# A graph layer on one core: the order of fills, stores, loads and tests in the head of the kernel

## The chip, the core and the metric

The kernel runs on one core of one Trainium2 chip. A core has five engines that each work through their own list of instructions in order: TensorE (PE in the profile), VectorE (DVE), ScalarE (ACT), GpSimd (POOL) and SyncE (SP). SP, ACT and POOL also issue DMA transfers; an issue that has to wait holds up everything behind it in its engine's list. The metric is the device time of one execution in microseconds (us). Three runs of the kernel before gave 2591.33, 2595.76 and 2597.96 us: median 2595.76.

## The reference

There are 12500 nodes with 64 features and 212500 edges, sorted by their node dst (E = 212500, N = 12500). Cut to what matters:

```
h = max(layernorm(x), 0)
e = silu(concat(h[src], h[dst], w) @ eW1 + eb1)     # an edge: 129 inputs, 128 outputs
e = silu(e @ eW2 + eb2)
agg = segment_sum(e, src, 12500)
out = x + silu(concat(h, agg) @ nW1 + nb1) @ nW2 + nb2
```

The first product is split: h @ eW1[:64] and h @ eW1[64:128] are formed once per node. The kernel calls the first table A (`ta`, by the node src, in three bf16 parts) and the second B (`tb`, by the node dst, in f32).

## The kernel before, in words

**Two halves that run beside each other.** The edges are dealt to 100 buckets by src (`NB`; bucket = src mod 100, 125 nodes each). The *sending* half takes the edges in their own order, in blocks of 1024 (208 blocks), forms for each the B row plus weight and bias (a product of a one-hot matrix `pick` with a window `win` of B's rows, lines 341 to 356), and scatters the rows to DRAM tensors `q` by bucket: eight indirect DMAs a block, issued by POOL (line 370), 1661 in all. The *step* half reads `q` bucket by bucket (line 415), adds the rows of A (line 420), does both layers and the sums per node (lines 438 to 516). The blocks are grouped in eleven chunks (`CHUNKS`); chunk 0 has eight blocks, each other chunk twenty. A chunk has its own tensor `q`, and the steps of a chunk start when all its blocks are sent. Unused places of `q` must read zero; `fill` (line 91) writes them from the tile `zeros` (line 88), in four transfers a chunk, issued by ACT at line 100.

**Order.** The order of PE, DVE, ACT and SP is the order of the code (`manual_schedule`); only POOL's is not. Work that shall run side by side is written as generators that give way after each piece. `turns(todo, 3)` runs up to three of them in turn. `send_all(c)` (line 381) sends a chunk: for each block s it loads for s + 2, issues a fill of the next chunk while there are any, and then takes three pieces of `count(s + 1)` and `send(s)` together. After each piece of chunk 0 the loop around it takes four steps of `feed`: twelve a block.

**Loads of a block (SP).** `load_rows(s)` loads `bc` (line 265; the dst row of each edge, one row broadcast to 64 partitions) and `bb` (line 267; the bucket of each edge) from the tensor `rows`. `load(s)` first calls `load_rows(s + 1)` and then loads the two halves of the window `win` (line 281), at rows that SP reads from `base_i`. `weights(s)` loads the edge weights into a row of `pick` (line 292), after DVE has written the rest of `pick`. `count(s)` (DVE) makes `pick` and the one-hot `oh` (lines 306, 307) and the running counts (lines 317, 322); `send(s)` has PE's products, two copies to `qs` by ACT (line 356), the targets `to` by DVE (line 361), and the scatters.

**The head**, before the first block is sent (lines 711 to 745):
- SP loads `x0` (the first 2048 rows of x) and `srcR`; ACT loads `dstR`.
- ACT issues the first of four fills of chunk 0; the other three are issued one after each of the next pieces of `norm(x0)` (lines 532 to 544: mean, `cen`, Square on ACT, var, Sqrt on ACT, then max and scale), `destinations()` (`f` from `dstR` by ACT, line 619; `lo`; `rowsS`; a store to `rows`, line 632) and `sources()` (`sf` from `srcR` by ACT, line 642; the bucket by DVE, lines 644 to 647; a second store to `rows`, line 650).
- `load_rows(0)`; then the transposes of the buckets to `bkE` and `first_rows(g)` four times: the rows of B of the first 2048 nodes, copied to `got` (line 183, three buffers) and stored to `tb0` by SP (line 565). Block windows below 30 read `tb0`.
- `scale(0)` (lines 670 to 673) turns buckets into target rows for chunk 0.
- `load(0)`, `load(1)`, the transposes of `locE`, and then all of `count(0)` with `weights(0)`.
- `feed` is `checks()` and after it `turns(groups(), 3)`. `checks()` tests that each window holds all rows that its block needs (lines 679 to 683, two reduces over `f`) and then scales the buckets of chunks 1 to 10, one `scale(c)` each: twelve steps in all. `groups()` makes A and B for all nodes, twelve buckets at a time: `loaded` (line 570, x into `xs`), `normed` (the norm above), and `products` of four buckets each.

Of the kernel before, what the change touches and what calls it, by code (L numbers as in the profile page):

```python
# [46 lines left out]
G = 4  # L47
# [12 lines left out]
def tile_gnn(ctx: ExitStack, tc: tile.TileContext, x, src, dst, ew, eW1, eb1, eW2, eb2, nW1, nb1, nW2, nb2, out):  # L60
# [25 lines left out]

    most_zeros = max((cap * P - zero) * G * W // 64 for _, cap, zero in CHUNKS)
    zeros = const.tile([P, most_zeros], F32, name="zeros")
    nc.gpsimd.memset(zeros, 0.0)

    def fill(c, engine, each):

# [71 lines left out]

    ta = dram.tile([P * NB, 3 * H], BF16, name="ta")
    tb = dram.tile([P * NB, H], F32, name="tb")
    rows = dram.tile([NP, 2, 2, BLK], BF16, name="rows")

    tb0 = dram.tile([P * NE, H], F32, name="tb0")
    ta_buckets, tb_buckets = (t.rearrange("(l b) f -> l b f", b=NB) for t in (ta, tb))  # L170
# [68 lines left out]
    with ExitStack() as work:  # L239
# [18 lines left out]
        def load_rows(s):  # L258

            if s < nblocks:  # L260
                p, g = s // 2, s % 2
                r = rows[p, g]
                bc = ld.tile([P, HALF], BF16, name="bc")
                of = bass.AP(tensor=r.tensor, offset=r.offset, ap=[[HALF, 2], [0, HB], [1, HALF]])
                nc.sync.dma_start(bc, of)
                bb = ld.tile([P, BLK], BF16, name="bb")
                nc.sync.dma_start(bb[:112], bass.AP(tensor=r.tensor, offset=r.offset + BLK, ap=[[0, 112], [1, BLK]]))
                blk[s] = [bc, bb]

        def load(s):  # L270

            load_rows(s + 1)
            if s < nblocks:
                p, g = s // 2, s % 2
                win = wins[s % NW]
                table, end = (tb0, NE * P) if s < EARLY else (tb, N)
                assert s < EARLY or len(done_b) == NB // G
                for a in range(2):
                    h = 2 * g + a
                    at = nc.sync.value_load(base_i[:, h, p : p + 1], min_val=0, max_val=end - WL)  # L280
                    nc.sync.dma_start(win[a * HB : a * HB + WL, :], table[bass.ds(at, WL), :])
                pick = ld.tile([P, HALF], F32, name="pick")
                blk[s] += [win, pick]

        def weights(s):

# [45 lines left out]
        def send(s):  # L332

            p, g = s // 2, s % 2
            c = chunk_of[s]
            _, _, cap, _, q = chunks[c]
            _, _, win, pick, run = blk.pop(s)
# [14 lines left out]
            halves = []  # L352
            for t0 in range(0, nt, G):
                qs = qsp.tile([P, G, W], F32, name="qs")
                m = min(G, nt - t0)
                nc.scalar.copy(qs[:, :m, :H], qps[t0 // G][:, :m, :])  # L356
                halves.append((t0, m, qs))
            for t0, m, qs in halves:
                if t0 == 0:
                    to = top.tile([P, TB], I32, name="to")  # L360
                    nc.vector.scalar_tensor_tensor(
                        to[:, :nt], rank[:, :nt], float(G * cap * P), bkE[:, g * TB : g * TB + nt, p], op0=OP.min, op1=OP.add
                    )
                at = g * TB + t0
                nc.scalar.copy(
                    qs[:, :m, H:], locE[:, at : at + m, p][:, :, None].to_broadcast([P, m, W - H])
                )
                for t in range(t0, t0 + m):
                    k = min(P, n - t * P)
                    i = nc.gpsimd.indirect_dma_start(  # L370
                        out=q[:],
                        out_offset=bass.IndirectOffsetOnAxis(ap=to[:k, t : t + 1], axis=0),
                        in_=qs[:k, t - t0, :],
                        in_offset=None,
                    )
# [182 lines left out]
        def first_rows(g):  # L558

            hr = turned(x0, g)  # L560
            yield
            got = fp.tile([P, G, H], F32, name="got")
            product(1, hr, mm, "mm", got)
            yield
            nc.sync.dma_start(tb0.rearrange("(p j) f -> p j f", j=NE)[:, g : g + G, :], got)
            yield

        def loaded(b0, n, xs):
# [48 lines left out]
        def destinations():  # L617

            nc.scalar.copy(f, dstR)
            lim = lp.tile([NP, 1], F32, name="lim")  # L620
            nc.vector.tensor_scalar(lim, part[:NP], EARLY / 2 - 0.5, float(N - NE * P), op0=OP.is_gt, op1=OP.mult)
            nc.vector.tensor_scalar(lim, lim, float(NE * P - WL), None, op0=OP.add)
            yield
            nc.vector.tensor_scalar(lo, fv[:, :, 0], lim, None, op0=OP.min)
            for g in range(2):
                nc.vector.tensor_tensor(
                    rowsS[:, g, 0, :].rearrange("p (a e) -> p a e", a=2),
                    fv[:, 2 * g : 2 * g + 2, :],
                    lo[:, 2 * g : 2 * g + 2, None].to_broadcast([NP, 2, HALF]),
                    op=OP.subtract,  # L630
                )
            nc.sync.dma_start(rows[:, :, 0, :], rowsS[:, :, 0, :])
            yield
            lot = mm.tile([1, 4, NP], F32, name="lot", tag="mm")
            for g in range(4):
                nc.tensor.transpose(lot[:, g, :], lo[:, g : g + 1], ident[:NP, :NP])
            nc.scalar.copy(base_i, lot)
            yield

        def sources():  # L640
# [6 lines left out]
            nc.vector.scalar_tensor_tensor(sf, t, -float(NB), sf, op0=OP.mult, op1=OP.add)  # L647
            yield
            nc.scalar.copy(rowsS[:, :, 1, :], sf.rearrange("p (g e) -> p g e", g=2))
            nc.sync.dma_start(rows[:, :, 1, :], rowsS[:, :, 1, :])  # L650
            yield

        def by_edges(of, to):
# [8 lines left out]
                    nc.scalar.copy(to[:, k0 : k0 + 4, :], tr)  # L662
                yield

        def scale(c):
            p0, p1, cap, _, _ = chunks[c]
            v = bkE[:, :, p0:p1]

            q4 = lp.tile([P, 2 * TB, p1 - p0], F32, name="q4", tag=f"q4{c > 0}")
            nc.vector.tensor_scalar(q4, v, 0.5 - G / 2, 1.0 / G, op0=OP.add, op1=OP.mult)  # L670
            nc.vector.tensor_scalar(q4, q4, float(3 * 2**22), None, op0=OP.add)
            nc.vector.tensor_scalar(q4, q4, -float(3 * 2**22), None, op0=OP.add)
            nc.vector.scalar_tensor_tensor(v, q4, float(cap * P * G - G), v, op0=OP.mult, op1=OP.add)

        def checks():

# [4 lines left out]
                nc.vector.tensor_scalar(ends[:, i, :], ends[:, i, :], sign, limit, op0=OP.mult, op1=OP.is_gt)  # L681
                yield
            nc.vector.tensor_reduce(bad[:NP, 0:1], ends.rearrange("p i g -> p (i g)"), AX.X, OP.max)
            for c in range(1, len(chunks)):
                scale(c)
                yield

        def groups():
# [5 lines left out]
            for i, b0 in enumerate(starts):  # L694
                if i + 2 < len(starts):
                    todo.append((b0, loaded(*of[i + 2])))
                todo += [(b0, products(b0, g, of[i][2])) for g in range(0, size(b0), G)]
                if i + 1 < len(starts):
                    todo.insert(len(todo) - size(b0) // G + 1, normed(*of[i + 1]))
            return todo  # L700

        done_a, done_b, ready = [], [], set()
# [9 lines left out]
        with tc.tile_pool(name="lists", bufs=1, side="right") as lp:  # L712
# [12 lines left out]
                    queue.dma_start(to[p0:p1, :], vec(v, p0 * PAIR, p1 - p0, PAIR))  # L725
                queue.dma_start(to[NP - 1 : NP, :LAST], vec(v, (NP - 1) * PAIR, 1, LAST))
            nc.scalar.dma_start(dstR[NP - 1 : NP, LAST:], vec(dst, E - PAD, 1, PAD))
            zero_fills = list(fill(0, nc.scalar, 7))
            zero_fills.pop(0)()
            steps_ = [norm(x0, NE), destinations(), sources()]  # L730
            for _ in turns(steps_, 3):
                if zero_fills:
                    zero_fills.pop(0)()
            load_rows(0)
            counting = count(0)
            for i, _ in enumerate(turns([by_edges(sf, bkE)] + [first_rows(g) for g in range(0, NE, G)], 3)):
                if i == 8:
                    scale(0)
            for i in range(2):
                load(i)  # L740
            for _ in by_edges(t, locE):
                pass
            for _ in counting:
                pass
            feed = itertools.chain(checks(), turns(groups(), 3))
            for _ in send_all(0):
                for _ in range(4):
                    next(feed, None)
# [203 lines left out]
```

## Time and profile before

| what | value |
|---|---|
| three runs | 2591.33, 2595.76, 2597.96 us (median 2595.76) |
| the profiled execution | 2590.2 us |
| its span | 2588.4 us, 60017 instructions |
| PE, DVE, ACT, POOL busy, share of the span | 85%, 79%, 48%, 67% |
| first scatter of block 0, 1, 2 | 63.71, 83.64, 97.01 us |
| last scatter | 2339.2 us |
| bytes moved by DMA | 577.23 MB, 223 GB/s over the span |
| POOL idle ahead of scatters, "issue" | 397.5 us in 1302 waits |
| DVE's `to` waiting for scatters | 149.3 us in 81 waits |

A line of the timeline gives start and length in us, the engine (a q behind it marks a DMA issue or the like by that engine's sequencer), the source line, the operation, the tile written and the tiles read, the shapes, a count, and in brackets the idle time of the engine just before with what ended it. A line of the waits gives who waited for what: us in total, times, and the longest. A line of busy time by stretch gives the stretch, its length, the busy us of PE, weight load, DVE, ACT and POOL with instruction counts, the clock granted to PE, the busy share of the DMA engines, and GB/s.

### The profile page before, as it was taken

Reading aid. Unit: us, or ns where it says so; the run is one execution under the profiler, and the core shown is the slowest. Engines: PE = TensorE matmul, PEld = TensorE weight load, DVE = VectorE, ACT = ScalarE, POOL = GpSimd, SP = SyncE. Lnnn points to the kernel's source line nnn. Section 1 sums busy time; section 2 is a strip of 40 time slices with the busy share of each in tenths; the row PEclk is TensorE's granted clock in tenths of the full one; section 3 lists DMA queues with packets and bytes.
Section 4 is the critical chain, followed back from the end, with each engine's and each line's share of the span. In section 5 each row is a group of like instructions: output and inputs, shape, how many; then the busy total and the mean of one; then the engine's idle time right before and its main releaser. Section 6 shows DMA issues by size and latency. Waiting matters only on the chain.

```text
span 2588.4 us, 60017 instructions
## 1 busy us (share of the span) xinstructions
PE 2205.0 (85%) x21814; PEld 2041.8 (79%) x21814; DVE 2034.8 (79%) x3464; ACT 1246.9 (48%) x2687; POOL 1736.8 (67%) x1729
## 2 busy tenths in 40 slices
PE   2456777988998998999899799889889999997997
PEld 1345667977987987888788799889879889996996
DVE  5877987987987887888788799879879889973442
ACT  2344634544554554555455455445545455553443
POOL 3675777777777777777677777777767777772000
PEclk7556888998999999999999899999989999998999
DMA  8787778669768767866966877786696667655441
GB/s 202 216 246 263 254 234 271 217 204 269 237 210 247 252 219 227 267 216 218 272 227 211 240 248 237 220 260 228 211 274 228 215 203 235 230 169 174 166 150 54
DMA packets 257977, 577.23 MB, mean 223 GB/s; under 512 B 51202, under 2 KB 110580, under 8 KB 257469
## 3 DMA queue, kind: packets, MB, share of 16 engines
q1 hardware_dynamic: 185096, 384.91, 45.7%
q0 software_dynamic: 54144, 123.04, 13.1%
q10 hardware_dynamic: 18434, 65.37, 11.4%
q8 instruction: 175, 2.87, 0.5%
q14 instruction: 128, 1.04, 0.1%
HBM read 361.44 MB, written 211.67 MB: 221 GB/s over the span
## 4 chain that ended last, share of the span: by engine, by line
PE 40%; DMA 23%; DVE 13%; POOL 7%; issue 6%; ACT 2%; SPq 1%; DVEq 0%; ACTq 0%; POOLq 0%
DMA q<-qs,to 14%; PE seg L505 10%; PE p L491 9%; POOL q L370 7%; PE pt L459 7%; PE pt L452 5%; DVE misc L317 5%; PE qp L349 4%; PE lr L438 3%; DMA bc<-rows 2%; DVE oneT L443 2%; DMA bb<-rows 2%; DVE one L472 2%; DMA pick<-in_edge_weight_dram 2%; DVE own L322 2%
## 5 line engine op out<-in xcount | busy, mean ns | idle before, releaser
L370 POOL DMA_INDIRECT q<-qs,to x1661 | 1697.4, 1022 | 602.7 <-issue 397.5
L463 ACT ACTIVATE e<-pt 128x512 f32<-128x512 f32 x525 | 313.7, 598 | 835.8 <-PE pt L459 769.6
L505 PE MATMUL seg<-one,e 128*128 128x125 f32 x4200 | 581.4, 282 | 54.7 <-DVE aggT L516 42.5
L491 PE MATMUL p<-w,e 128*128 128x128 f32 x4200 | 587.2, 284 | 5.3 <-ACT p L485 5.3
L317 DVE TENSOR_TENSOR_SCAN misc<-oh,misc 100x342 f32<-100x342 f16 (+1 forms) x623 | 579.7, 930 | 9.3 <-PE misc L341 1.2
L505 PEld LDWEIGHTS seg<-one,e 128*128 128x128 f32 x4200 | 524.4, 196 | 68.5 <-ACT p L485 27.7
L491 PEld LDWEIGHTS p<-w,e 128*128 128x128 f32 x4200 | 527.9, 197 | 31.0 <-issue 8.4
L443 DVE TENSOR_SCALAR oneT<-lr,part 125x512 bf16<-125x512 f32 x525 | 390.8, 744 | 111.1 <-PE lr L438 109.0
L459 PE MATMUL pt<-oneT,a 125*128 125x256 bf16 (+1 forms) x3300 | 443.0, 273 | 0.1
L452 PE MATMUL pt<-ident,qt 128*128 128x128 f32 x2100 | 332.0, 282 | 73.4 <-DVE oneT L443 73.4
L356 ACT COPY qs<-qp 128x512 f32<-128x512 f32 x416 | 229.2, 587 | 320.3 <-PE qp L349 225.7
L472 DVE TENSOR_TENSOR one<-nodes,qt 128x500 f32<-128x500 f32 x525 | 351.7, 670 | 0.7 <-PE seg L505 0.5
L459 PEld LDWEIGHTS <-a 125*128 125x128 bf16 x3300 | 318.7, 100 | 35.5 <-issue 1.0
L322 DVE TENSOR_TENSOR own<-misc,oh 100x342 f16<-100x342 f32 (+1 forms) x623 | 320.0, 514 | 21.6
L495 ACT ACTIVATE e<-p 128x512 f32<-128x512 f32 x525 | 314.1, 598 | 18.6 <-PE p L491 18.0
L485 ACT COPY p<-b2f 128x512 f32<-128x512 f32 x525 | 312.5, 595 | 0.1
L349 PE MATMUL qp<-win,pick 50*128 50x128 f32 x3322 | 260.7, 299 | 60.6 <-DMA pick<-in_edge_weight_dram 34.5
L349 PEld LDWEIGHTS qp<-win,pick 50*128 50x128 f32 x3322 | 220.4, 200 | 92.9 <-issue 71.5
L452 PEld LDWEIGHTS pt<-ident,qt 128*128 128x128 f32 x2100 | 228.3, 144 | 79.0 <-DVE oneT L443 76.3
L516 DVE TENSOR_TENSOR aggT<-aggT,seg 128x500 f32<-128x500 f32 x250 | 166.9, 667 | 94.2 <-PE seg L505 93.9
L438 PE MATMUL lr<-identb,qt 128*125 128x128 bf16 x2100 | 213.3, 225 | 30.6 <-DMA qt<-q 25.3
L438 PEld LDWEIGHTS <-qt 128*125 128x125 bf16 x2100 | 186.4, 139 | 42.1 <-DMA qt<-q 31.5
(121 smaller groups left out, 1086.3 us busy)
## 6 DMA issues: line engine op xcount, KB each, us to landing
qt<-q SPq DMA_DIRECT2D x250, 576.0 KB
a<-ta SPq DMA_DIRECT2D x275, 384.0 KB
q<-zeros ACTq DMA_DIRECT2D x30, 1638.0 KB
bb<-rows SPq DMA_DIRECT2D x208, 224.0 KB
bc<-rows SPq DMA_DIRECT2D x208, 128.0 KB
q<-qs,to POOLq DMA_INDIRECT x1661
win<-tb SPq DMA_DIRECT2D x416, 24.0 KB
ta<-parts SPq DMA_DIRECT2D x25, 384.0 KB
```

The lines of the kernel that those rows point to most:

```text
L317: nc.vector.tensor_tensor_scan(run[:, :m], oh[:, cols], nil.to_broadcast([NB, m]), carry.get(c, -1.0), op0=OP.add, op1=OP.add)
L322: nc.vector.tensor_tensor(own[:, cols], run[:, :m], oh[:, cols], op=OP.mult)
L349: nc.tensor.matmul(qps[a][:, t, :], pick[half, t * P : (t + 1) * P], win[half, :], start=True, stop=True)
L370: i = nc.gpsimd.indirect_dma_start(out=q[:], out_offset=bass.IndirectOffsetOnAxis(ap=to[:k, t : t + 1], axis=0), in_=qs[:k, t - t0, :], in ...
L438: nc.tensor.matmul(lr[:L, t, :], loc[:, at : at + 1].to_broadcast([P, L]), identb, start=True, stop=True)
L443: nc.vector.tensor_scalar(oneT, st[k].pop("lr")[:L], part1[:L, :], None, op0=OP.is_equal)
L452: nc.tensor.matmul(pt[:, t, :], qt[:, j, :H], ident, is_transpose=True, start=t == 0, stop=False, skip_group_check=True)
L459: nc.tensor.matmul(pt[:, cols, :], a3[:L, b, i, :], oneT[:, cols, :], start=False, stop=i == 2, skip_group_check=True)
L472: nc.vector.tensor_tensor(one.rearrange("p (b j) l -> p b j l", j=n), nodes1[:, None, None, :].to_broadcast(wide), loc[:, tiles[0][1] : ti ...
L491: nc.tensor.matmul(p2[:, t, :], e1[:, t, :], w2, start=False, stop=t == G - 1, skip_group_check=True)
L495: nc.scalar.activation(e2, p2, AF.Silu)
L505: nc.tensor.matmul(item[2][:, b, :], e2[:, t, :], one[:, t, :], start=j < G, stop=j >= G * (n - 1))
```

## The change

It has these parts:
1. `zeros` is set by VectorE instead of GpSimd.
2. The four fills of chunk 0 are all issued by ACT ahead of the norm of `x0`.
3. The rows of B of the first nodes (`tb0`) are stored by ACT instead of SP.
4. The tensor `rows` becomes two: `dests` (read as `bc`) and `bucks` (read as `bb`).
5. `load(s)` loads the window first and calls `load_rows(s + 1)` after it, in every block. In the head, all of `count(0)`, with `weights(0)`, now comes between `load(0)` and `load(1)`.
6. `checks()` is no longer ahead of the groups of nodes, but one of their generators, queued behind the products of the first twelve buckets. The ten scales of chunks 1 to 10 become one (those chunks have the same capacity), with one point at which it gives way: four steps instead of twelve. An assertion at build time makes sure that a chunk is scaled before it is sent.

```diff
-    nc.gpsimd.memset(zeros, 0.0)
+    nc.vector.memset(zeros, 0.0)
...
-    rows = dram.tile([NP, 2, 2, BLK], BF16, name="rows")
+    dests = dram.tile([NP, 2, BLK], BF16, name="dests")
+    bucks = dram.tile([NP, 2, BLK], BF16, name="bucks")
...
         def load(s):
-            load_rows(s + 1)
             if s < nblocks:
...
                     nc.sync.dma_start(win[a * HB : a * HB + WL, :], table[bass.ds(at, WL), :])
                 pick = ld.tile([P, HALF], F32, name="pick")
                 blk[s] += [win, pick]
+            load_rows(s + 1)
...
         def first_rows(g):
...
-            nc.sync.dma_start(tb0.rearrange("(p j) f -> p j f", j=NE)[:, g : g + G, :], got)
+            nc.scalar.dma_start(tb0.rearrange("(p j) f -> p j f", j=NE)[:, g : g + G, :], got)
...
-            nc.sync.dma_start(rows[:, :, 0, :], rowsS[:, :, 0, :])
+            nc.sync.dma_start(dests, rowsS[:, :, 0, :])
...
-            nc.sync.dma_start(rows[:, :, 1, :], rowsS[:, :, 1, :])
+            nc.sync.dma_start(bucks, rowsS[:, :, 1, :])
...
-        def scale(c):
-            p0, p1, cap, _, _ = chunks[c]
+        def scale(cs):
+            p0, p1, cap = chunks[cs[0]][0], chunks[cs[-1]][1], chunks[cs[0]][2]
             v = bkE[:, :, p0:p1]
-            q4 = lp.tile([P, 2 * TB, p1 - p0], F32, name="q4", tag=f"q4{c > 0}")
+            q4 = lp.tile([P, 2 * TB, p1 - p0], F32, name="q4", tag=f"q4{cs[0]}")
             nc.vector.tensor_scalar(q4, v, 0.5 - G / 2, 1.0 / G, op0=OP.add, op1=OP.mult)
             nc.vector.tensor_scalar(q4, q4, float(3 * 2**22), None, op0=OP.add)
+            yield
             nc.vector.tensor_scalar(q4, q4, -float(3 * 2**22), None, op0=OP.add)
             nc.vector.scalar_tensor_tensor(v, q4, float(cap * P * G - G), v, op0=OP.mult, op1=OP.add)
+            scaled.update(cs)
...
         def checks():
...
-            for c in range(1, len(chunks)):
-                scale(c)
+            for _, cs in itertools.groupby(range(1, len(chunks)), lambda c: chunks[c][2]):
+                yield from scale(list(cs))
                 yield
...
         def groups():
...
+                if i == 0:
+                    todo.append(checks())
...
-            zero_fills = list(fill(0, nc.scalar, 7))
-            zero_fills.pop(0)()
-            steps_ = [norm(x0, NE), destinations(), sources()]
-            for _ in turns(steps_, 3):
-                if zero_fills:
-                    zero_fills.pop(0)()
+            for f_ in fill(0, nc.scalar, 7):
+                f_()
+            for _ in turns([norm(x0, NE), destinations(), sources()], 3):
+                pass
             load_rows(0)
             counting = count(0)
...
-                    scale(0)
-            for i in range(2):
-                load(i)
+                    list(scale([0]))
+            load(0)
+            for _ in counting:
+                pass
+            load(1)
             for _ in by_edges(t, locE):
                 pass
-            for _ in counting:
-                pass
-            feed = itertools.chain(checks(), turns(groups(), 3))
+            feed = turns(groups(), 3)
             for _ in send_all(0):
                 for _ in range(4):
                     next(feed, None)
```

More of the change, by code (lines that the diff above doesn't have):

```diff
@@ L261, in load_rows @@
                 p, g = s // 2, s % 2
-                r = rows[p, g]
+                r, r2 = dests[p, g], bucks[p, g]
                 bc = ld.tile([P, HALF], BF16, name="bc")
@@ L266, in load_rows @@
                 bb = ld.tile([P, BLK], BF16, name="bb")
-                nc.sync.dma_start(bb[:112], bass.AP(tensor=r.tensor, offset=r.offset + BLK, ap=[[0, 112], [1, BLK]]))
+                nc.sync.dma_start(bb[:112], bass.AP(tensor=r2.tensor, offset=r2.offset, ap=[[0, 112], [1, BLK]]))
                 blk[s] = [bc, bb]
         def load(s):
-            load_rows(s + 1)
             if s < nblocks:
@@ L336, in send @@
             _, _, cap, _, q = chunks[c]
+            assert c in scaled
             _, _, win, pick, run = blk.pop(s)
@@ L699, in groups @@
                     todo.insert(len(todo) - size(b0) // G + 1, normed(*of[i + 1]))
+                if i == 0:
+                    todo.append(checks())
             return todo
-        done_a, done_b, ready = [], [], set()
+        done_a, done_b, ready, scaled = [], [], set(), set()
         feeding = ExitStack()
```

## The prediction

> **What bounds the kernel now.** I read the page's busy times first, then its costliest groups, then busy time by stage, then the timeline of the head.
>
> ```profile
> PE 2205.0 (85%) x21814; PEld 2041.8 (79%) x21814; DVE 2034.8 (79%) x3464; ACT 1246.9 (48%) x2687; POOL 1736.8 (67%) x1729
> ...
> L370 POOL DMA_INDIRECT q<-qs,to x1661 | 1697.4, 1022 | 602.7 <-issue 397.5
> ```
>
> POOL looks loosely used at 67%. But nearly all of it is 1661 scatters of 1.02 us, and two thirds of its idle time is "issue": about 0.30 us ahead of each scatter for which nothing in the profile is to blame. One scatter therefore holds POOL 1.32 us. The stretches (columns: length, then PE, PEld, DVE, ACT, POOL busy with counts, PE clock, DMA share, GB/s):
>
> ```profile
> 82.70:155.70 73.00, 46.93 (x347) 37.76 (x349) 64.08 (x113) 37.78 (x103) 54.04 (x51) 0.50 0.77 235
> 155.70:254.00 98.30, 50.78 (x455) 43.77 (x453) 63.70 (x108) 44.42 (x112) 60.00 (x57) 0.60 0.81 252
> 254.00:2340.00 2086.00, 1861.26 (x18943) 1739.81 (x18941) 1762.74 (x2980) 1040.78 (x2235) 1575.43 (x1545) 0.96 0.73 232
> 2340.00:2588.00 248.00, 228.09 (x1951) 205.89 (x1951) 95.34 (x157) 103.18 (x204) 19.03 (x26) 0.96 0.43 140
> ```
>
> From 254 us on, 1545 instructions x 1.32 fill 2040 of 2086 us: POOL is full, and a microsecond by which the scatters start earlier or later there stays to the end. So the change is worth what it does to the scatters of the head. Three lines of POOL's timeline (start, length, [idle before, what ended it]) are the first scatters of blocks 0, 1 and 2:
>
> ```profile
> 63.71 1.05 POOL L370 DMA_INDIRECT q<-qs,to  x1 [23.73 <-ACT qs L365]
> 83.64 1.22 POOL L370 DMA_INDIRECT q<-qs,to  x1 [9.92 <-DVE var L543]
> 97.01 0.96 POOL L370 DMA_INDIRECT q<-qs,to  x1 [3.01 <-ACT qs L365]
> ```
>
> Then blocks 3 to 8 follow at 10.6 to 11.1 us without a gap (108.10, 118.79, 129.58, 140.63, 151.73). What each part touches, from the timeline of all engines:
>
> ```profile
> 12.35 1.06 ACT L536 ACTIVATE x<-cen 128x1024 f32<-128x1024 f32 x1 [0.84 <-DVE cen L535]
> 15.66 2.32 ACTq L100 DMA_DIRECT2D q<-zeros  x1
> 18.08 1.90 ACT L642 CAST sf<-srcR 104x2048 f32<-104x2048 int32 x1 [0.54 <-issue]
> 39.41 4.77 SPq L565 DMA_DIRECT2D tb<-got  x4
> 43.17 0.65 ACT L183 COPY got<-ab 128x256 f32<-128x256 f32 x2 [7.51 <-DMA tb<-got]
> 55.86 0.60 SPq L292 DMA_DIRECT2D pick<-in_edge_weight_dram  x1
> 77.16 0.95 DVE L532 TENSOR_REDUCE mean<-xs 128x12 f32<-128x768 f32 x1 [2.82 <-DMA xs<-in_x_dram]
> 104.46 0.16 DVE L361 SCALAR_TENSOR_TENSOR to<-misc,bkE 128x8 int32<-128x8 f32 x1
> ```
>
> **Zeros on VectorE.** 936 numbers a row. The nearest DVE row, srcR's 492 in 0.47 us, gives 0.9 us; DVE then idles 7.4 us for x, which hides it (0.9 us if that cover were gone). srcR's own memset, and the two small pieces of src behind it, come 0.9 us later; the 768 KB piece does not wait for it. POOL gains 0.88 us and idles 23.7 us ahead of its first scatter. Zero.
>
> **All four fills ahead of the norm.** The first goes at 9.47, when the loads have begun to land; the others stand between ACT's steps and take 0.58, 0.61 and 2.32 us to issue. The DMA engines are full meanwhile:
>
> ```profile
> 10.00:15.00 5.00, 0.00 (x0) 0.00 (x0) 4.67 (x15) 3.72 (x4) 1.75 (x4) 1.00 1.02 257
> 25.00:30.00 5.00, 3.51 (x20) 3.20 (x22) 1.18 (x1) 3.39 (x5) 2.64 (x6) 1.00 1.00 208
> ```
>
> With a share of 1.0 from 5 to 35 us, the bytes cannot land sooner for being asked for sooner. ACT, however, works in order: the line at 18.08 starts when the fourth issue has ended (15.66 + 2.32 = 17.98). With all four first, the Square of line 536 waits for them. Bounds for the end of the fourth: 9.47 + 0.66 + 0.58 + 0.61 + 2.32 = 13.6 us, if only issue time counts, and 18.0, if the queue takes the fourth only when enough of the first has drained, which the same full DMA decides. I take 18.0, the row itself. Then table load 1.28, Square 1.06, reduce and scale 1.4, Sqrt 0.21, f's cast 1.90: f is ready at 24.1 instead of 17.5, and everything behind it (sf, bkE, rows of B) comes 6.5 us later (2.2 by the lower bound): the last product of rows of B ends at 43.1, not 36.5.
>
> **Rows of B stored by ACT; lists in two tensors.** Now the four stores stand on SP behind bb, which waits for the second list, so ACT loses 7.51 us waiting for a got buffer. On ACT the first store goes at about 39 and the fourth got needs no wait: 43.1 to 43.8, store issued by 44.5, landed 2.4 later as now (44.18 to the first window at 46.57). Windows start at 46.9: +0.3. The gain of 7.5 and the loss of 6.5 cancel. Splitting the lists is worth nothing, since the two loads already wait apart:
>
> ```profile
> SPq L265 <- DMA rows<-rowsS: 6.2, 1, 6.2
> SPq L267 <- DMA rows<-rowsS: 3.1, 1, 3.1
> ```
>
> (If bc were held by both, the first wait would have ended with the second.) [...]
>
> **Block 0 before block 1.** From the first window SP needs 2.5 us for two windows and 1.2 for bc and bb; then block 0's weights go at 50.6 instead of 55.86: -5.3. Landing took 4.25 (to 60.12), and 3.6 more led to the first scatter: 58.4, if nothing else stood before it.
>
> **Tests moved.** Something does. The feed gives four steps after each piece. Today block 0's three pieces take the twelve steps of the tests; without these, the first four are loads of xs0 and xs1, then mean, cen and Square, then var and Sqrt, and all stand ahead of block 0's qs copies on ACT and of its to on DVE. This wait now falls on block 1: mean at 77.16 waits for xs, the scatter follows 6.5 us later. In the change xs0 is issued at 46.9 + (64.86 - 46.57) - 4.83 (the loads of 60.03 to 64.86, which come later) = 60.4. Landing has bounds 3.8 us (a 256 KB store, 39.41 to 43.17) and 12.3 (64.86 to 77.16, beside a 1638 KB fill); I take 5, near the first, as the earlier fill is through by 57 and the next stands behind the Square. Mean at 65.4, block 0 scattered from **71.9 instead of 63.7**. With the steps of blocks 1 and 2 shifted to 0 and 1: block 1 at 71.9 + 13.4 = 85.3 (now 83.64), block 2 at + 11.1 = 96.4 (now 97.01). The head is even there, at -0.6.
>
> The tests themselves then meet block 2: two reduces with their small ones 2 x 2.6, and one scale of 128x1600 instead of ten of 128x160. By L644 (2048 in 1.23) and L647 (2.29) that is 3 x 0.97 + 1.8 = 4.7; in all 10.1 us instead of 17.3. Today they run while DVE has little else. In block 2, DVE has 12% idle (64.1 of 73), and to is only 1.5 to 3.6 us ahead of POOL (104.46 to 108.10, 117.28 to 118.79). So block 3 is late by 10.1 - 1.3 - about 3 = 6; bounds 0 (all in gaps) and 10. POOL cannot win that back. But the feed stays 8 steps ahead, and in 155.7 to 254, where POOL loses 98 - 57 x 1.32 = 23 us, some comes back: 0 to 4, I take 2.
>
> **Window loads before bc and bb, in all 208 blocks.** The weights now follow bc directly. bc took from 35.26 to 41.88 alone, pick 4.25. Weights wait at most until bc is through: 0 to 2.5 us a block (two windows fewer between them, as above); cover is the block of 10.7 us until qp. Where SP is held at bb, the earlier windows save up to the same: -2.5 to +2.5 a time. Taken as +0.6 in all. [...]
>
> **Sum.** -0.6 + 6 - 2 + 0.6 = **+4 us** on the profiled execution: 2590.2 + 4 = 2594. That execution lies 5.6 under the median of the runs, 2595.8, so I predict **2600 us** on the runs' scale.
>
> **Rivals.**
> (1) Faster: xs lands 3.8 us after an issue at 58, block 0 starts at 68, block 1 follows back to back at 78.6 and block 2 at 89.4 (-7.6); the tests fit DVE's 8.9 idle us, and 4 come back later: -12, 2584. For: the waits of 9.92 and 3.01 lie in the row. Against: DVE's order is nearly POOL's pace there.
> (2) Slower: the weights behind bc. "DMA pick" is 2% of the chain of waits (52 us). If each of some ten such waits, one a chunk, grows by 2.5 us, that is +25; half of it, 12, on top of the forecast gives 2612. It decides where weights land later than 10 us after bc. Against: PE waits for pick only 34.5 us in 12 times.
> (3) The fills gain nothing, the stores as much as the fills lose, and the change does not shorten the head: this is the forecast.
>
> **How the numbers follow.** About 0.3% (7.8 us) is what a measurement can tell from no change. Forecast 2600 (2588 to 2604 is "the same"): 0.42. Rival 1, below 2588: 0.22. Rival 2, or tests that cost their whole 10 us, above 2604: 0.36. The range leaves out about 0.1 at either end: 2581 to 2616.
>
> **What would show it.** Four fills back to back, with the Square at about 19; first window near 47; weights at 51; xs's mean before the first scatter, which starts at 72; a gap of POOL of some 6 us at block 3, beside DVE's reduce over f. I am wrong if the Square stays near 12, if the first scatter comes before 64, if the reduces meet an idle DVE, or if the gaps of 155 to 254 change by more than 4 us.

## The result and the profile after

The changed kernel took 2609.36 us (median of six runs, 2605.29 to 2614.36), the kernel before 2592.56 (2590.14 to 2597.96): ratio 1.0069, 95% interval 1.0056 to 1.0083. The change makes the kernel 17 us **slower**. The time lies inside the range, but not where the forecast put it (2600, no measurable change). The profiled execution of the changed kernel is the slowest of its six, 2614.36 us with a span of 2612.2; against the profiled execution of before (2590.2) that is 24 us, not 17. In the new file most line numbers are one to five higher (the scatter is L372, the Square L538, the reduces of the tests L684).

The page of the changed kernel, busy time and the scatters:

```profile
PE 2200.6 (84%) x21814; PEld 2044.6 (78%) x21814; DVE 2030.9 (78%) x3429; ACT 1245.5 (48%) x2685; POOL 1755.2 (67%) x1728
...
L372 POOL DMA_INDIRECT q<-qs,to x1661 | 1716.5, 1033 | 608.3 <-issue 404.1
```

The engines do the same work, and the scatters are the same 1661. They are 19 us longer in sum than in the profile of before, but that is not the loss: from block 48 on they are 17 us longer and the idle time between them 13.5 us shorter, and f_stores below, with 9 us more of scatters, loses nothing. Busy time by stretch (same columns as before) still shows POOL full from 254 us on (1585.1 us busy and 1536 x 0.30 us idle ahead of its instructions fill 2046 of 2086), and fuller DMA engines from 82 us (0.82, 0.83 and 0.77, against 0.76, 0.81 and 0.73 before):

```profile
82.00:155.70 73.70, 35.49 (x287) 30.34 (x288) 62.59 (x104) 32.88 (x89) 52.29 (x49) 0.52 0.82 236
155.70:254.00 98.30, 50.79 (x382) 40.54 (x382) 62.35 (x106) 40.35 (x105) 56.40 (x55) 0.53 0.83 242
254.00:2340.00 2086.00, 1855.03 (x18956) 1740.98 (x18956) 1768.86 (x2991) 1041.85 (x2239) 1585.11 (x1536) 0.95 0.77 233
```

The head of the changed kernel, from the timeline of all engines (start, length, engine, line; in brackets the idle time before, and what ended it):

```profile
9.59 8.66 ACTq L100 DMA_DIRECT2D q<-zeros  x4
...
19.58 1.06 ACT L538 ACTIVATE x<-cen 128x1024 f32<-128x1024 f32 x1
...
47.12 0.60 ACTq L100 DMA_DIRECT2D q<-zeros  x1
...
47.47 1.47 SPq L281 DMA_DIRECT2D win<-tb  x2
48.98 2.01 SPq L266 DMA_DIRECT2D bc<-dests  x1
...
53.22 1.95 SPq L293 DMA_DIRECT2D pick<-in_edge_weight_dram  x1
...
60.02 0.55 DVE L307 TENSOR_SCALAR pick<-bc,same,plus 128x512 f32<-128x512 bf16 x1 [10.75 <-DMA bc<-dests]
62.97 1.67 SPq L572 DMA_DIRECT2D xs<-in_x_dram  x4
...
70.61 0.95 DVE L534 TENSOR_REDUCE mean<-xs 128x12 f32<-128x768 f32 x1 [9.43 <-DMA xs<-in_x_dram]
```

The four fills hold ACT to 18.25 and the Square comes at 19.58, as forecast. The first windows come at 47.47, also as forecast. Then it slips: the first fill of chunk 1 (47.12) now stands just ahead of block 1's bc (48.98), which lands only at 60.0; DVE waits 10.75 us for it. The load of xs is issued at 63.0 and has landed at 70.6. The scatters, from POOL's timeline (first of blocks 0, 1, 2, 3 and 10):

```profile
77.21 1.19 POOL L372 DMA_INDIRECT q<-qs,to  x1 [37.38 <-ACT qs L367]
...
90.32 0.96 POOL L372 DMA_INDIRECT q<-qs,to  x1 [2.17 <-ACT qs L367]
...
102.12 0.96 POOL L372 DMA_INDIRECT q<-qs,to  x1 [1.00 <-ACT qs L367]
...
117.69 0.96 POOL L372 DMA_INDIRECT q<-qs,to  x1 [3.51 <-ACT got L184]
...
204.60 0.96 POOL L372 DMA_INDIRECT q<-qs,to  x1 [10.33 <-issue]
```

Block 0 starts after the mean (6.6 us behind it), not ahead of it; block 3 has a gap ahead of it that it did not have; block 10 has one of 10.3 us, where the kernel before has 4.2 (at block 11 it is the other way: 5.6 against 9.6). The table gives the start of a block's first scatter minus the same start in the kernel before, for the changed kernel and for the four experiments that ran at the same pace (told below). All are single profiled executions; the two last rows are from all runs of a kernel, against the kernel before on the same chip.

| block | changed | f_load | f_tests | f_stores | c_xs |
|---|---|---|---|---|---|
| 0 | +13.5 | +10.1 | +6.2 | -3.5 | -4.7 |
| 1 | +6.7 | +3.3 | +5.5 | -0.1 | -7.0 |
| 2 | +5.1 | +1.0 | +5.2 | -0.3 | -9.8 |
| 4 | +10.8 | +6.1 | +8.0 | -0.1 | -9.4 |
| 9 | +9.6 | +4.7 | +9.1 | 0.0 | -8.6 |
| 13 | +15.2 | +8.7 | +11.3 | -0.6 | -9.6 |
| 23 | +12.9 | +6.8 | +7.3 | -2.8 | -10.8 |
| 48 | +21.1 | +12.2 | +13.4 | -0.3 | -5.6 |
| last scatter | +24.6 | +13.8 | +13.7 | -0.7 | +0.1 |
| median of the runs | +16.8 | +9.3 | +12.9 | -2.1 | -6.0 |
| 95% interval of the ratio, in us | 14.5 to 21.5 | 6.2 to 13.7 | 9.9 to 21.0 | -4.2 to 2.3 | -9.9 to -3.9 |

The experiments whose labels begin with u_, n_ or h_ ran on two chips on which the kernel before itself takes 3585 and 3464 us and POOL does not set the pace; none of their times is compared with one of the others. The granted clock of TensorE is no rival for the loss of the changed kernel (0.919 in its profile): f_stores was granted 0.925 in its profile and loses nothing.

### The profile page after: what moved, and what is told of

Its sections match the earlier page's. It is cut to its first block, busy times and chain, and to the rows that moved or that the text cites. A ratio compares the mean times of both kernels' runs of the same rounds, so it can differ in the third digit from the quotient of the medians.

```text
span 2612.2 us, 60000 instructions
## 1 busy us (share of the span) xinstructions
PE 2200.6 (84%) x21814; PEld 2044.6 (78%) x21814; DVE 2030.9 (78%) x3429; ACT 1245.5 (48%) x2685; POOL 1755.2 (67%) x1728
## 3 DMA queue, kind: packets, MB, share of 16 engines
q10 hardware_dynamic: 19010, 66.42, 11.1%
## 4 chain that ended last, share of the span: by engine, by line
PE 48%; DMA 15%; DVE 14%; POOL 6%; issue 5%; SPq 1%; ACT 1%; DVEq 0%; ACTq 0%; POOLq 0%
PE seg L507 12%; PE p L493 11%; DMA q<-qs,to 10%; PE pt L461 8%; PE pt L454 6%; POOL q L372 6%; PE qp L351 5%; DVE misc L318 5%; PE lr L440 3%; DVE oneT L445 2%; DVE one L474 2%; DMA pick<-in_edge_weight_dram 2%; DVE own L323 2%; DVE aggT L518 1%; DMA win<-tb 1%
## 5 line engine op out<-in xcount | busy, mean ns | idle before, releaser
L372 POOL DMA_INDIRECT q<-qs,to x1661 | 1716.5, 1033 | 608.3 <-issue 404.1
L497 ACT ACTIVATE e<-p 128x512 f32<-128x512 f32 x525 | 314.7, 599 | 11.9 <-PE p L493 11.3
```

What stands on the lines that cost most here:

```text
L372: i = nc.gpsimd.indirect_dma_start(out=q[:], out_offset=bass.IndirectOffsetOnAxis(ap=to[:k, t : t + 1], axis=0), in_=qs[:k, t - t0, :], in ...
L497: nc.scalar.activation(e2, p2, AF.Silu)
```

## The experiments

The theories: **T1**, the move of the tests (part 6) is the main cost. **T2**, the order of the loads (part 5). **T3**, the fills at once (part 2). **T4**, the stores by ACT (part 3) gain time by themselves. The first four kernels each undo one part of the change.

The group of scatters in u_tests shows that POOL is not full on the two chips named above:

```profile
L372 POOL DMA_INDIRECT q<-qs,to x1661 | 1674.8, 1008 | 1578.5 <-ACT qs L367 836.3
```

The scatters are no longer than elsewhere, but POOL idles 1578.5 us ahead of them (608.3 in the changed kernel), 836.3 of it put down to ACT's copies to qs. In n_tests, on the second chip, POOL is busy 1126.3 us from 254 to 2340 us (1585.1 in the changed kernel). From 254 to 2340 us the clock granted to TensorE is 0.81 there and 0.82 in n_tests, and 0.95 in the profile above. Over the span the eight profiles of these two chips show 0.809 to 0.852, the other six 0.919 to 0.935. The lower clock alone does not explain times that are 34 and 38% longer (0.95 / 0.81 is 1.17, if all work went with the clock), and from 254 to 2340 us TensorE is busy 1652.5 us in u_tests, less than the 1861.3 before; what else slows these chips stays open, and that TensorE sets the pace there, as the expectations of f_load, f_tests and f_stores have it, is not shown. TensorE has little to do in the head (busy 14.4 of the first 60 us in u_tests and in n_tests), and the first scatters of one kernel on the two chips agree within 1.5 us; so the heads of these runs are used, their times decide nothing.

**u_tests**: tests ahead of the groups again (and the one scale is ten again, not shown).

```diff
-                if i == 0:
-                    todo.append(checks())
...
-            feed = turns(groups(), 3)
+            feed = itertools.chain(checks(), turns(groups(), 3))
```

> The changed kernel with one part undone: the tests of the lists (and the ten scales) are taken ahead of the groups of nodes again, as before the change. T1 (the move of the tests is the main cost): the norm of the first group of nodes no longer stands ahead of block 0's qs and to, so its first scatter comes at about 65 instead of 77.2; block 3 has no gap of 3.5 us ahead of it; 5 to 11 us of the 17 come back, 2598 to 2604 us. T2 (the order of the loads) and T3 (the fills) leave the tests no part in it: the first scatter may come earlier, but block 2 stays at 100 to 103, the steps of +5 to +6 at block 10 and of +3 at blocks 30 and 48 stay, and the time stays at 2606 to 2612.

Measured: 3559.58 against 3584.60, ratio 0.9928 (0.9900 to 0.9955). Blocks 0 and 1 at 71.7 and 90.9: the first scatter is 5.5 us earlier than in the changed kernel, block 1 is not. That is neither forecast: T1 is right on block 0 only, and there in direction (about 65 was said).

**u_fills**: fills paced between the pieces of the norm again.

```diff
-            for f_ in fill(0, nc.scalar, 7):
-                f_()
-            for _ in turns([norm(x0, NE), destinations(), sources()], 3):
-                pass
+            zero_fills = list(fill(0, nc.scalar, 7))
+            zero_fills.pop(0)()
+            for _ in turns([norm(x0, NE), destinations(), sources()], 3):
+                if zero_fills:
+                    zero_fills.pop(0)()
```

> The changed kernel with one part undone: the four fills of chunk 0 are paced between the pieces of the norm again. T3 (the fills at once hold up the head): Square at 12.4 instead of 19.6, the first window at about 41 instead of 47.5, first scatter 6 us earlier (71), and since POOL is full from there, about 6 us less in all, 2603. T1 and T2 (the loss comes later, or from the loads): the head gains its 6 us, but block 3 still waits for the tests and block 10 for its weights, so that less than 3 us arrive at the end, 2606 to 2610.

Measured: 3553.60, ratio 0.9907 (0.9876 to 0.9938). Square at 13.0, but the first windows only at 46.5, not 41: what ACT gains at 13 us does not reach the windows. Block 0 still starts 3.7 us earlier (73.6).

**u_load**: bc and bb of block s + 1 ahead of the window of block s again.

```diff
         def load(s):
 
+            load_rows(s + 1)
             if s < nblocks:
...
                 blk[s] += [win, pick]
-            load_rows(s + 1)
```

> The changed kernel with one part undone: the rows bc and bb of block s + 1 are loaded ahead of the window of block s again, in all blocks and in the head. T2 (order of the loads): bc of block 1 is issued before the fill of chunk 1 and lands after some 6 us instead of 11; the shifts at block 10 (+6), 30 (+3), 48 (+3.5) and 138 (+2.5) of the changed kernel against the one before are gone, and with them some 10 us: 2597 to 2600. T1 and T3: the shifts after block 9 come from the late start and not from the order of the loads, and stay; 2606 to 2611.

Measured: 3590.02, ratio 1.0000 (0.9973 to 1.0028). bc of block 1 is issued at 40.1, ahead of the fill at 46.5, and block 0 starts at 72.9, as T2 said; the later blocks can't be read on that chip.

**u_stores**: the stores of the rows of B on SP again (`nc.scalar.dma_start(tb0...` becomes `nc.sync.dma_start(tb0...`).

> The changed kernel with one part undone: the four stores of the rows of B stand on SP again. T4 (the move of the stores pays by itself): with the lists late, they stand behind bb in SP's order, ACT waits 7 us or more for a got buffer, the windows come 6 to 8 us later than 47.5, and the time rises by as much, 2614 to 2617. Rival: the late start is hidden behind the wait for xs and for the tests, so that the time stays within 3 us of the changed kernel's, 2606 to 2612.

Measured: 3569.82, ratio 0.9950 (0.9926 to 0.9974). The four stores take SP from 38.3 to 43.9, ACT waits only 1.6 us for a got buffer, and the first windows come at 46.2. That is 38.0 us after the first fill (8.2), as in the changed kernel (9.6 and 47.5: 37.9), not 6 to 8 us later. T4 falls, as far as the head goes.

**n_tests, n_load, n_fills**: the kernels u_tests, u_load and u_fills on the second of these chips.

> The same kernel as u_tests (tests and ten scales ahead of the groups of nodes again), because u_tests ran where TensorE was granted 0.82 and the kernel before took 3585 us, so that POOL was not what bounds it. Where the kernel before takes about 2593: T1 (move of the tests): first scatter at 66 to 72 as in u_tests (71.7), block 3 without a gap of 3.5 us, 5 to 11 of the 17 us gone, a ratio of 1.002 to 1.005. T2 (order of the loads): 1.006 to 1.008, since the shifts at blocks 10, 30, 48 and 138 stay.

> The same kernel as u_load (bc and bb of block s + 1 ahead of the window of block s again), for the same reason. Where the kernel before takes about 2593: T2: first scatter 4 us earlier than 77.2, as in u_load (72.9), and the shifts of the changed kernel against the one before at block 10 (+6), 30 (+3), 48 (+3.5) and 138 (+2.5) gone: a ratio of 1.000 to 1.003. T1 and T3: these shifts stay, 1.005 to 1.008.

> The same kernel as u_fills (the four fills paced between the pieces of the norm again), for the same reason. Where the kernel before takes about 2593: T3: the 3.7 us by which its first scatter came earlier in u_fills (73.6 against 77.2) reach the end, a ratio of 1.005 or less. T1 and T2: block 3 or block 10 takes them back, 1.006 to 1.008.

Measured against 3464.17: 0.9980 (0.9950 to 1.0009), 0.9990 (0.9953 to 1.0026), 1.0001 (0.9972 to 1.0031). No difference shows beyond these intervals, and those of up to 0.9% on the first chip do not come again. But the heads repeat: block 0 at 71.6, 74.3 and 73.6. How the fills reach block 0 is seen in the timeline of n_fills:

```profile
42.55 0.60 ACTq L100 DMA_DIRECT2D q<-zeros  x1
...
48.97 2.03 SPq L266 DMA_DIRECT2D bc<-dests  x1
...
56.07 0.55 DVE L307 TENSOR_SCALAR pick<-bc,same,plus 128x512 f32<-128x512 bf16 x1 [5.24 <-DMA bc<-dests]
...
60.24 2.15 SPq L572 DMA_DIRECT2D xs<-in_x_dram  x4
...
67.04 0.95 DVE L534 TENSOR_REDUCE mean<-xs 128x12 f32<-128x768 f32 x1 [9.79 <-DMA xs<-in_x_dram]
...
73.64 1.19 POOL L372 DMA_INDIRECT q<-qs,to  x1 [33.79 <-ACT qs L367]
```

bc of block 1 is issued at the same time as in the changed kernel (48.97), but the fill of chunk 1 went 4.6 us earlier, and bc is there at 56.1 instead of 60.0. The mean of xs and block 0 behind it are 3.6 us earlier. In all seven kernels in which this bc goes out behind that fill, DVE gets it 12.9 to 13.5 us after the *fill's* issue, whenever bc itself was issued (1.9 to 6.8 us behind the fill). So the fills of chunk 0 cost through the *next* chunk's fill, which ACT issues when it is through with its head. The step from bc to the load of xs, which is 2.7 us earlier here, is read from the timelines and was not tested by itself.

**h_stores**: tests, fills and load order undone together; the zeros by VectorE, the stores by ACT, the two tensors and the head's order of block 0 before block 1 remain.

> The tests, the fills and the order of bc and the windows are as before the change; what is left of it are the zeros by VectorE, the rows of B stored by ScalarE, the two tensors of lists, and in the head block 0's rows ahead of block 1's. T4 (the stores pay by themselves, once the lists are not late): no wait of 7.5 us of ACT for a got buffer, the first window at 41 instead of 46.6, weights 0 at about 47 instead of 55.9, first scatter at 56 to 58 instead of 63.7, and xs 6 us earlier, so that block 1 follows at 77 to 78 and block 2 at 91: 3 to 6 us faster than the kernel before, a ratio of 0.9975 to 0.999. Rival: bc of block 0 and the chunk-1 fill, not the stores, set the windows and the landing of xs; blocks 1 and 2 keep 83.6 and 97, ratio 0.999 to 1.001.

Measured: 3465.91, ratio 0.9989 (0.9961 to 1.0017). Blocks 0, 1, 2 at 60.5, 83.6, 97.9: the rival's numbers, T4 falls.

**f_load**: the kernel u_load, on a chip where the kernel before takes 2593.58.

> The same kernel as u_load and n_load, again, because both ran where the kernel before took 3464 to 3585 us and TensorE, not POOL, set the pace, so that they can't decide. Where the kernel before takes about 2593, T2 (order of bc and the windows in all 208 blocks) has the steps of +5 at block 10, +4 at block 30, +3.5 at block 48 and +2.5 at block 138 gone: last scatter at 2349 or earlier, ratio 1.000 to 1.003. T1 (tests and late start, and what follows from them) has them stay: last scatter 2356 to 2362, ratio 1.005 to 1.008.

Measured: **2602.88**, ratio 1.0039 (1.0024 to 1.0053). Between the two forecasts. Its head:

```profile
40.21 0.55 SPq L266 DMA_DIRECT2D bc<-dests  x1
...
50.41 0.54 DVE L307 TENSOR_SCALAR pick<-bc,same,plus 128x512 f32<-128x512 bf16 x1
...
63.33 1.69 SPq L572 DMA_DIRECT2D xs<-in_x_dram  x4
...
67.20 0.95 DVE L534 TENSOR_REDUCE mean<-xs 128x12 f32<-128x768 f32 x1 [15.85 <-DMA xs<-in_x_dram]
...
73.81 1.19 POOL L372 DMA_INDIRECT q<-qs,to  x1 [34.37 <-ACT qs L367]
```

DVE no longer waits for block 1's bc (no bracket at 50.41), and xs lands 3.9 us after its issue, not 7.6. Block 0 is 3.4 us earlier than in the changed kernel, and at block 9 the difference is 4.9. The step of +6 at block 10 stays, and so do those of blocks 3 and 30. The order of the loads is worth 16.8 - 9.3 = 7.5 us, of which 4.9 are made by block 9. T2 is right on the head and wrong on block 10. Why xs lands sooner with this order is not shown.

**f_tests**: the kernel u_tests, where the kernel before takes 2593.59.

> The same kernel as u_tests and n_tests (tests and ten scales ahead of the groups of nodes again), again, since both ran where TensorE set the pace. f_load has left +10 to +14 of the shift in place, with a step of +6 at block 10. Where the kernel before takes about 2593: T1 (what is left comes from the move of the tests): first scatter at 71.6, block 3 without its gap, shift at block 4 no more than +5 instead of +10.8, no step at block 10, and 9 to 11 of the 17 us gone: ratio 1.002 to 1.004. Rival (the late start of everything, by the fills and by bc of block 1, is what block 10 pays for): the first scatter moves to 71.6 but block 1 waits for xs to about 90.8, as in u_tests and n_tests, the shift stays at +7 or more to block 9 and at +12 or more behind block 10, and the ratio at 1.005 to 1.007.

Measured: **2606.50**, ratio 1.0060 (1.0038 to 1.0081): the rival's number, though its shift of +12 behind block 10 is reached only at block 48. With the tests undone only about 4 of 17 come back, less than the intervals can tell from nothing; T1, which said 9 to 11, falls as the main cost. The timeline says why:

```profile
45.84 0.60 ACTq L100 DMA_DIRECT2D q<-zeros  x1
...
50.35 2.00 SPq L266 DMA_DIRECT2D bc<-dests  x1
...
58.79 0.55 DVE L307 TENSOR_SCALAR pick<-bc,same,plus 128x512 f32<-128x512 bf16 x1 [7.70 <-DMA bc<-dests]
59.86 2.28 DVE L684 TENSOR_REDUCE ends<-f 104x4 f32<-104x2048 f32 x1
...
82.62 0.95 DVE L534 TENSOR_REDUCE mean<-xs 128x12 f32<-128x768 f32 x1
...
89.10 1.22 POOL L372 DMA_INDIRECT q<-qs,to  x1 [9.12 <-ACT qs L367]
```

With bc behind the fill, DVE's pick for block 1 waits, and the tests wait behind it: they begin at 59.9 (in h_stores, with the old order of the loads and the fills paced, at 50.4), the mean at 82.6, and block 1 comes at 89.1 with or without them. Block 2 lasts 11.1 us (102.2 to 113.3), as before the change; in the changed kernel and in f_load, with the tests in it, 15.6 and 16.0. So the tests do cost 4.5 to 5 us where they were put; undoing them brings little, because the other parts make the head late by themselves, and because f_tests loses 4 us of its own from block 3 to block 8 (+5.2 to +9.3).

**c_xs**: a version from what these showed: h_stores with one scale instead of ten, taken between block 0's first and second piece, and xs loaded before block 0. The edit below is against h_stores; `scale` is as in the change.

```diff
-            feed = itertools.chain(checks(), turns(groups(), 3))
+            making = turns(groups(), 3)
+            for _ in range(2):
+                next(making)
+            tests = checks()
+            feed = itertools.chain(itertools.islice(tests, 2), [None] * 2, tests, [None] * 8, making)
```

> h_stores (tests, pacing of the fills and order of bc and the windows as before the change) with two edits. The loads of xs for the first two groups of nodes are issued at the end of the head, ahead of block 0, instead of in block 1; and the ten scales become one, as in the change, but between block 0's first and second piece, behind its to. The other steps of the feed stay where they stood. In h_stores the first scatters of blocks 0, 1 and 2 came at 60.5, 83.6 and 97.9, and the mean of block 1 waited for xs until 77.2. Theory (block 1 waits for the norm of the first group, and that for xs and for DVE's scales): mean at 67 to 70 without a wait for xs, block 1 from 73 to 77, block 2 from 86 to 90, 6 to 9 us less than the kernel before, which stay to the end where POOL sets the pace: 2584 to 2588 us where the kernel before takes 2593.6, ratio 0.9965 to 0.998. Rival (something else holds block 1, or the loads of xs delay bc and the weights of blocks 1 and 2 by as much): block 1 stays at 80 to 84, block 2 at 95 to 98, ratio 0.999 to 1.002.

Measured: **2586.72** against 2592.71, ratio 0.9974 (0.9962 to 0.9985): faster than both kernels. Its timeline:

```profile
56.77 1.70 SPq L572 DMA_DIRECT2D xs<-in_x_dram  x4
...
65.28 0.95 DVE L534 TENSOR_REDUCE mean<-xs 128x12 f32<-128x768 f32 x1
...
76.66 1.30 POOL L372 DMA_INDIRECT q<-qs,to  x1 [5.84 <-ACT hr L557]
...
87.22 0.97 POOL L372 DMA_INDIRECT q<-qs,to  x1 [0.30 <-ACT got L184]
```

The mean waits for nothing, block 1 comes 7.0 us and block 2 9.8 us earlier than before the change. So the norm of the first group, and with it xs and DVE's scales, did hold block 1; how much of it was xs and how much the ten scales was not separated. Of the 9 to 10 us, 6 are left in the medians; in the profiled execution (2589.47, among the slower of its twelve) the last scatter is level with before.

**f_stores**: the kernel h_stores, where the kernel before takes 2594.74.

> The same kernel as h_stores (of the change only the zeros, the stores of the rows of B, the two tensors of lists, and block 0's rows ahead of block 1's in the head), again, since that ran where TensorE set the pace. There block 1 came at 83.6 and block 2 at 97.9, as in the kernel before. In f_load, f_tests and c_xs the time is 3 to 5 us more than their shift at block 9 (5, 9 and -9 us against +9, +13 and -6 in the medians). Theory A (these four small parts cost something in every block, the two tensors of lists most likely): this kernel, with a head even with that of before, is 3 to 5 us slower, ratio 1.001 to 1.002. Theory B (they cost nothing; the 3 to 5 us depend on how the sending and the steps fall together): shift of 0 to 2 us at block 9, ratio 0.9990 to 1.0007.

Measured: **2592.65**, ratio 0.9996 (0.9984 to 1.0009): theory B. The four parts that are left of the change together make no difference that can be told from nothing; the loss sits in the fills, the loads and the tests (with their scales). The fills alone were not timed where POOL sets the pace. If the parts simply added, 16.8 + 2.1 - 7.5 - 3.9 = 7.5 us would be left for them and for what they do together; the head gives them 3.6.

## What the prediction had right and wrong, step by step

The time lies inside the range, but not for the reasons of the sum, which said +4 us and "no measurable change" (0.42). The range reached to 2616 because of rival 2 and of tests that cost their whole 10 us; neither is what happened (the tests cost 4.5 to 5, and for rival 2 see below), so that the time lies inside is luck. What failed is the start of the head (fills, loads, landing of xs: 5.2 us late) and "some comes back" (+5.6 instead of -2).

- **Fills.** The end of the fourth at 18.0 (measured 18.25), the Square at about 19 (19.58) and f at 24.1 (24.13; the terms listed add up to 23.9) were right; that the queue takes the fourth only when enough of the first has drained was the author's assumption, and no run shows it. "The gain of 7.5 and the loss of 6.5 cancel" was right for the first window (46.9; 47.47) and wrong as a price: zero was put where n_fills, with the new order of the loads, shows 3.6 us. It followed ACT up to the windows and not to ACT's next DMA, the fill of chunk 1: that came 1.8 us later (45.3 before), and with the new order of the loads it stands right ahead of block 1's bc, which before went out 1 us ahead of it (44.2).
- **Stores.** 7.5 us of ACT's wait went, as said. But in f_stores, where the fills are paced, another wait came in its place: by the profile ACT's second store is held until a fill has landed.

```profile
37.71 0.37 ACTq L567 DMA_DIRECT2D tb<-got  x1
38.13 0.37 ACT L557 COPY hr<-ht 128x256 f32<-128x256 f32 x1 [3.92 <-DMA q<-zeros]
```

Its last store is issued by 43.1, 1 us earlier than before (44.2), and the windows, which wait for the stores to land (SP's wait for them is 6.4 us in the changed kernel), come 5.4 us after that and not 2.4: at 48.6, against 46.6. The sum priced the move at ACT's wait, 7.5 us; measured with three other parts is 2.1 us in 2593, not to be told from nothing. The interval (-4.2 to 2.3) leaves no room for 7.5 by the four parts together.
- **Block 0 before block 1.** Weights 0 at 50.6 forecast, 53.2 measured: SP's issues of bc and bb took 2.0 and 2.1 us behind the fill, not 1.2 together. The landing of xs at 5 us was 7.6 (inside the bounds of 3.8 and 12.3; in f_load it is 3.9). Together the mean came at 70.6 instead of 65.4, the whole error of the head.
- **The tests.** That the norm then stands ahead of block 0 was right: mean to scatter 6.6 us (6.5), block 1 13.1 later (13.4), block 2 11.8 later (11.1). Only its start was 5.2 late: +5.1 at block 2 instead of -0.6. "Block 3 late by 6" was nearly right: from +5.1 at block 2 to +9.6 at block 3 and +10.8 at block 4; the gap itself is 3.5 us, not 6.
- **"Some comes back", -2.** This failed in sign. Between blocks 9 and 13 the changed kernel loses 5.6 more. POOL's idle times just ahead of blocks 10 to 13 add up to 26.1 us there and to 20.2 before. (POOL's busy time from 155.7 to 254 fell by 3.6 us, just under the 4 that were to be the sign of being wrong.) ACT's timeline of the changed kernel ahead of block 10:

```profile
186.93 0.84 ACT L538 ACTIVATE xs<-cen 128x768 f32<-128x768 f32 x1 [2.93 <-DVE cen L537]
199.69 0.58 ACTq L100 DMA_DIRECT2D q<-zeros  x1
200.31 0.21 ACT L543 ACTIVATE var<-var 128x12 f32<-128x12 f32 x1 [12.54 <-DMA pick<-in_edge_weight_dram]
```

and of the kernel before:

```profile
173.07 0.42 ACT L555 COPY hr<-ht 128x256 f32<-128x256 f32 x1
184.05 0.60 ACTq L100 DMA_DIRECT2D q<-zeros  x1
184.69 0.62 ACT L597 CAST parts<-rows_a 128x512 bf16<-128x512 f32 x1 [11.20 <-DMA ta<-parts]
...
188.30 0.96 POOL L370 DMA_INDIRECT q<-qs,to  x1 [4.17 <-ACT got L183]
```

Both times a fill on ACT's list goes out only after a wait of 11 to 12.5 us, and ACT is held with it; by the profile the wait ends when another transfer has landed (a load of weights; before, a store of A's rows). Before, a cast for A was behind it; now it is the norm's Sqrt, on which DVE waits too (11.1 us, to 200.6), and POOL has nothing for 10.3 us. The gap at block 10 is there in f_load (10.1 us) and smaller in f_tests (5.7), in both of which the loads or the tests are as before; ahead of blocks 10 to 13 together it is 24.6 and 22.5 us. It goes with the place that the tests' move gave the feed. That it is *this* order and not the later time alone was only argued.
- **Loads, +0.6.** Measured about 7.5 in the medians: 3.4 at block 0, 4.9 by block 9, the rest later. The bounds (-2.5 to +2.5 a block) were wide enough; missed was the head, where bc of block 1 changes places with a fill.
- **Rival 2** named nearly the right time (2612) by a wrong way: TensorE's wait for the weights is 45.0 us in 9 waits in the changed kernel (34.5 in 12 before), but 44.5 in 12 in f_load with the order undone. The order that puts the weights behind bc is not what makes them late.

The sum on profiled executions was -0.6 + 6 - 2 + 0.6 = +4. Measured to block 13: +5.1 + 5.7 - 1.2 + 5.6 = +15.2. That this is near the +16.8 of the medians is chance: in the same two executions the last scatter is 24.6 us later. What follows stays **open**: between blocks 23 and 48 the changed kernel loses 8.2, f_load 5.4, f_tests 6.1, c_xs 5.2 and f_stores 2.5, and no part was found for it; single executions of one kernel differ by as much (2605 to 2614).

## What to carry to other kernels

Where an engine is full from some point on, price a change of the head by when that engine gets its first pieces, and follow each delayed engine to its *next DMA issue*: here a small load that everything waits for was moved behind other loads, and fell 1.9 us behind a big transfer that it had been 1 us ahead of. When an independent task is moved out of a quiet stretch, look at what takes its place there: here a norm that waits for a load moved in ahead of the first block. Loading that input earlier and making one scale of ten, with the tests left where they hid, was worth 6 us.

## What the runs showed of the hardware

- A load of 128 KB that is spread to 128 partitions (bc) took 7.1 (n_fills), 8.4 (f_tests) and 11.0 us (changed kernel) until DVE had it, behind a fill of 1.6 MB issued 6.4, 4.5 and 1.9 us earlier on another engine's list. The time from the fill's issue is nearly the same: 13.5, 13.0 and 12.9 us (13.2 in u_fills, 13.0 in u_stores, 12.9 in u_tests and n_tests): the small load was in when some 13 us had passed since the fill. The bc of block 0, in the changed kernel, took 5.5 us with the last fill issued 19 us before (37.65 to 43.15); in n_fills, with the last of chunk 0's fills issued 17 us before, 9.0 (35.86 to 44.88). How long it takes with nothing else in flight is in no run.
- Issuing four fills back to back took ACT 8.66 us; with steps of the norm between them (n_fills) the four take 0.66, 0.58, 0.58 and 2.33. A store behind them on the same list was held 3.9 us (f_stores).
- The same kernel takes 2593 to 2595 us on some chips and 3464 and 3585 us on two others, at a granted clock of 0.92 to 0.96 and of 0.81 to 0.86 over the span; differences of 0.3% between these kernels can't be read there.
